# A two-layer graph network: host-laid edge lists and first weights, one load queue, the fallback branch at the end, products ahead of counts in the first row block

## The chip, the cores and the metric

The kernel runs on one core of a Trainium2 chip. The metric is the device time of one execution in microseconds; the median of three runs stands for the kernel. Profiles come from one further execution, whose own time is given beside its span.

## The reference

The inputs are 1250 nodes with 1024 features (x), 41250 edges (src, dst and one of two types; dst is sorted), and the weights. Two layers follow each other, each on h = relu(layernorm(x)) and each with a residual:

```python
h = max(layernorm(x), 0)
n = ln_weight * h * rsqrt(mean(h * h) + 1e-6)
y = n @ W_root + bias                          # 1024 x 286
for r in range(2):                             # two edge types
    w = (edge_type == r)
    y += segment_sum((n[src] @ W_rel[r]) * w, dst) / max(segment_sum(w, dst), 1)
x = x + h + elu(y) @ wo

h = max(layernorm(x), 0)
g = h @ W                                      # 1024 x 1024
e = exp(-leaky_relu((g @ a_l)[src] + (g @ a_r)[dst]))
x = x + elu(segment_sum(e * g[dst], src) / (segment_sum(e, src) + 1e-5))
```

## The kernel before

**Edges as counts.** Nothing is gathered. The edges, sorted by destination, are cut into NG = 110 chunks of J x 125 = 3 x 125 edges. Within a chunk the destinations span at most W = 16 nodes, so an edge is described by three numbers: the low seven bits of its source (`lows`), and a key that joins the source's tile of 128, the type, and the distance of its destination from the chunk's first one (`keys`). For each third of a chunk VectorE writes a one-hot matrix of the keys (`key`, line 505, 125 x 320); every second chunk it writes one of the low bits (`lo`, line 480). TensorE multiplies them (line 506) and so counts, in one PSUM bank for a chunk, the edges by source and by destination column. ScalarE copies the bank into the count matrix at a column that it loads from a table of first destinations (lines 511 to 513). An edge group that starts a new chunk at the previous chunk's last node is carried over by a small product (line 509) of one-hots `hot_ck` (line 487). Four PSUM banks serve the counts: three named `tp`, which the transposes share, and one of their own.

**Lists are prepared on the chip.** In `gnn_kernel` three loads of 110 rows x 375 entries come in on the queues of SP, ACT and POOL. VectorE finds each chunk's first and last destination, the step to the next chunk, and a number `odd` of chunks that break the assumption above; it forms keys, low bits and carries, and TensorE transposes them so that the edges of a chunk lie across partitions (lines 1204 to 1264). Then every engine loads `odd` into a register:

```python
n_odd = nc.values_load(info[0:1, NG:NG + 1], min_val=0, max_val=4 * NG + N)
with tc.If(n_odd == 0) as which:
    fast_arm(...)
with which.Else():
    general_arm(...)
```

The inputs here take the fast arm.

**Loads.** SP issues, after its list, x row block 0, then for each of 8 weight chunks the two relation matrices (one load) and the root matrix (another), with x row block 1 after chunk 3, then the other row blocks.

**Stage one of the fast arm.** The rows are cut into T = 10 blocks of 128. For a block t, `statistics` (line 528) and `norm` (line 541, ScalarE) form h, `turn` transposes eight tiles of it on TensorE (line 559), `scaled` copies them out of PSUM with the layer-norm weights (four on ScalarE, line 567, and four on VectorE, line 569), `square` (line 547) gives the second norm, `residual` adds h to x by a DMA of POOL. Sixteen products (line 648, 128 x 128 by 128 x 429, fp32, each two passes of the PE) take a block through two halves r of the three joined weight matrices, eight chunks k each. `first_part`, `second_part` and `third_part` bring the result of the block before to SBUF in three bf16 parts. The order on TensorE, VectorE and ScalarE is the program's own, since `manual_schedule` keeps them as written. Between two products `some(n)` advances the counts, so that all 330 key products are spread evenly over the 160 steps of the ten blocks:

```python
want = min(NG * J, ahead + -(-(NG * J - ahead) * (t * SK + i + 1) // (T * SK - 6)))
some(want - done)
```

Five of them (`ahead`) stand in front of the first product. In step i of block t stand also the preparation of blocks t + 1 and t + 2. The VectorE one-hots have five `key` buffers.

**Behind it** come the aggregation with the counts (line 719), the way back through wo (line 765), the second layer's product (lines 803 and 874), its edge weights (lines 947 and 950) and sums (lines 998 and 1011), and the output from line 969 on.

Of the kernel before, what the change touches and what calls it, by code (L numbers as in the profile page):

```python
# [30 lines left out]
J = 3  # L31
# [379 lines left out]
def fast_arm(tc, ctx, w_root, conv_bias, wo, w_gat, a_gat, out,  # L411
             ident, eps5, eps6, lnw, const, wt, wcat, bias, xs, cnt_raw,
             meta, keys, lows, hot_ck, ck, bases, iota_lo, iota_key, iota_ck):
# [56 lines left out]
    with ExitStack() as c1:  # L470
        hot = c1.enter_context(tc.tile_pool(name="hot", bufs=5))
        work = c1.enter_context(tc.tile_pool(name="work1", bufs=2))
# [17 lines left out]
        def chunks():  # L490

            for q in range(NG):
# [10 lines left out]
                for j in range(J):  # L503
                    key = hot.tile([PE_, 2 * T * W], BF16, name="key")
                    nc.vector.tensor_scalar(key, iota_key, keys[:, q, j:j + 1], None, op0=ALU.is_equal)  # L505
                    nc.tensor.matmul(acc[:, :2 * T * W], los[q // 2][:, :, (q % 2) * J + j], key, start=(j == 0),  # L506
                                     stop=(j == J - 1))
                    if q and j == 0:
                        nc.tensor.matmul(*carry, start=False, stop=False)
                    if j == J - 1:  # L510
                        b = nc.values_load(bases[0:1, q:q + 1], engines=[mybir.EngineType.Activation],
                                           min_val=0, max_val=N - 1)
                        nc.scalar.activation(cnt_w[:, :, bass.ds(b, W)], a3, AF.Copy)  # L513
                    yield
# [20 lines left out]
        def norm(t):  # L535
# [5 lines left out]
            nc.scalar.activation(h[:n], xs[t][:n], AF.Relu, bias=nmr[:n], scale=rstd[:n])  # L541
# [19 lines left out]
        def scaled(t, g):  # L561

            n, (hT, pts) = ROWS[t], hTs[t]
            for i in range(4):
                k = 4 * g + i
                if g == 0:
                    nc.scalar.activation(hT[:, k, :n], pts[g][:, i, :n], AF.Copy, scale=lnw[:, k:k + 1])
                else:
                    nc.vector.tensor_scalar(hT[:, k, :n], pts[g][:, i, :n], lnw[:, k:k + 1], None, op0=ALU.mult)
# [31 lines left out]

        for i in range(2):
            statistics(0, i)
        low_hots(0)
        carry_hots(0, 10)
        norm(0)
        some(4)
        for g in range(2):
            turn(0, g)
        scaled(0, 0)  # L610
        some(1)
        scaled(0, 1)
        done, ahead = 5, 5
        SK = 2 * KD
        for t in range(T):
            pys[t] = ps.tile([128, 2, 512], F32, name="mm")
            for i in range(SK):
                r, k = divmod(i, KD)
# [7 lines left out]
                if i == 6:  # L626
                    residual(t)
                if t == 0 and i in (1, 2):
                    statistics(1, i - 1)
                if t == 0 and i == 3:  # L630
                    norm(1)
                if t == 0 and i in (5, 7):
                    square(i // 6)
                if t + 2 < T:
                    if i in (6, 9):
                        statistics(t + 2, (i - 6) // 3)
                    elif i == 11:
                        norm(t + 2)
                    elif i == 13:
                        square(t + 2)  # L640
                if t + 1 < T:
                    if i in (8, 10):
                        turn(t + 1, i // 10)
                    elif i == 9:
                        scaled(t + 1, 0)
                    elif i == 12:
                        scaled(t + 1, 1)
                nc.tensor.matmul(pys[t][:ROWS[t], r, :F + HF], hTs[t][0][:, k, :ROWS[t]], wcat[k][:, r, :],  # L648
                                 start=(k == 0), stop=(k == KD - 1))
                want = min(NG * J, ahead + -(-(NG * J - ahead) * (t * SK + i + 1) // (T * SK - 6)))  # L650
# [459 lines left out]
def gnn_kernel(  # L1110
# [12 lines left out]
    a_gat: bass.AP,  # L1123
    out: bass.AP,
):
    nc = tc.nc
    D = x.shape[1]
    F = w_root.shape[1]
    HF = F // 2
    KD = D // 128  # L1130
    assert x.shape[0] == N and NG * GE == src.shape[0] and HF * 2 == F
# [4 lines left out]
    ident = const.tile([128, 128], F32, name="ident")  # L1136
    make_identity(nc, ident)
    ones = const.tile([128, 1], F32, name="ones")
    nc.vector.memset(ones, 1.0)
# [3 lines left out]
    nc.vector.memset(eps6, 1e-6)  # L1143
    lnw = const.tile([128, KD], F32, name="lnw")

    nc.scalar.activation(lnw[:, 0:1], eps5, AF.Sqrt)
    bias = const.tile([128, F], F32, name="bias")

    meta = const.tile([128, 2376], F32, name="meta")
    parts, at = [], 0  # L1150
    for size in (NG * J, NG * J // 2, NG * T, 3 * 128, T * W, T, NG, NG + 1):
# [5 lines left out]
    iota_lo = parts[3].bitcast(F16).rearrange("p (l j) -> p l j", j=2 * J)  # L1157
    iota_key, iota_ck, ck = parts[4].bitcast(F16), parts[5].bitcast(F16), parts[6]
    info = parts[7][0:1].bitcast(I32)

    xs = [big.tile([128, D], F32, name=f"x{t}", tag=f"x{t}") for t in range(T)]
    cnt_raw = big.tile([128, 2 * T * NPAD], F16, name="cnt")


    wt = [big.tile([128, D + 2], F32, name=f"w{k}") for k in range(KD)]
    wcat = [w[:, :3 * F].rearrange("p (r f) -> p r f", r=2) for w in wt]

    with ExitStack() as ec:
        ep = ec.enter_context(tc.tile_pool(name="ep", bufs=1))
        eps = ec.enter_context(tc.tile_pool(name="eps", bufs=2, space=PSUM))  # L1170
        eraw = ep.tile([NG, 3, GE], I32, name="eraw")
        for i, (a, eng) in enumerate(((dst, nc.sync), (src, nc.scalar), (etype, nc.gpsimd))):
            eng.dma_start(eraw[:, i, :], a.rearrange("(q e) -> q e", q=NG))
        lnw_row = ep.tile([KD, 128], F32, name="lnw_row")
        nc.scalar.dma_start(lnw_row, ln_w.rearrange("(k p) -> k p", p=128))
        nc.scalar.dma_start(bias, _bcast_rows(conv_bias, 128, F))

        def load_x(t):
            nc.sync.dma_start(xs[t][:ROWS[t]], x[t * 128:t * 128 + ROWS[t], :])

        load_x(0)
        for k in range(KD):
            ks = slice(k * 128, (k + 1) * 128)
            nc.sync.dma_start(wcat[k][:, :, :F], w_rel[:, ks, :].rearrange("r p f -> p r f"))
            nc.sync.dma_start(wcat[k][:, :, F:], w_root[ks, :].rearrange("p (r f) -> p r f", r=2))  # L1185
            if k == 3:
                load_x(1)
        for t in range(2, T):
            load_x(t)

        nc.gpsimd.iota(iota_lo, pattern=[[1, 128], [0, 2 * J]], base=0, channel_multiplier=0,
                       allow_small_or_imprecise_dtypes=True)
        nc.gpsimd.iota(iota_key, pattern=[[1, 2 * T * W]], base=0, channel_multiplier=0,
                       allow_small_or_imprecise_dtypes=True)
        nc.gpsimd.iota(iota_ck, pattern=[[1, 2 * T]], base=1, channel_multiplier=0,
                       allow_small_or_imprecise_dtypes=True)
        nc.gpsimd.memset(cnt_raw.rearrange("p (c n) -> p c n", n=NPAD)[:, :, N:], 0.0)


        end = ep.tile([NG, 1], F32, name="end")  # L1200
        nc.vector.tensor_scalar(end, ident[:NG, NG - 1:NG], N - 4096.0, 4096.0, op0=ALU.mult, op1=ALU.add)

        dstf = ep.tile([NG, GE], F32, name="dstf")
        nc.vector.tensor_copy(dstf, eraw[:, 0, :])
        first = ep.tile([NG, 1], F32, name="first")
        nc.vector.tensor_reduce(first, dstf, AX.X, ALU.min)
        below = ep.tile([NG, 1], F32, name="below")
        nc.vector.tensor_scalar_add(below, first, -4096.0)
        pn = eps.tile([128, 1], F32, name="pn", bufs=1)
        nc.tensor.matmul(pn[:NG], ident[:NG, 1:NG + 1], below, start=True, stop=True)  # L1210
        last = ep.tile([NG, 1], F32, name="last")
        nc.vector.tensor_reduce(last, dstf, AX.X, ALU.max)
        last2 = ep.tile([NG, 1], F32, name="last2")
        nc.vector.tensor_reduce(last2, dstf[:, :GE - PE_], AX.X, ALU.max)
        after = ep.tile([NG, 1], F32, name="after")
        nc.vector.tensor_tensor(after, pn[:NG], end, ALU.add)

        step = ep.tile([NG, 1], F32, name="step")
        nc.vector.tensor_tensor(step, after, first, ALU.subtract)
        odd = ep.tile([NG, 1], F32, name="odd")  # L1220
        nc.vector.tensor_scalar(odd, last, first, float(W), op0=ALU.subtract, op1=ALU.is_ge)
        nc.vector.scalar_tensor_tensor(odd, step, float(W), odd, op0=ALU.is_gt, op1=ALU.add)
        nc.vector.scalar_tensor_tensor(odd, last, after, odd, op0=ALU.is_gt, op1=ALU.add)
        nc.vector.scalar_tensor_tensor(odd, last2, after, odd, op0=ALU.is_ge, op1=ALU.add)
        pf = eps.tile([1, 128], F32, name="pf", bufs=1)
        nc.tensor.transpose(pf[:, :NG], first, ident[:NG, :NG])
        po = eps.tile([1, 1], F32, name="po", bufs=1)
        nc.tensor.matmul(po, odd, ones[:NG], start=True, stop=True)
# [73 lines left out]
```

## Time and profile before

| what | value |
|---|---|
| median of three runs | 631.08 us (630.55 to 632.11) |
| the profiled execution's time | 630.51 us |
| its span | 628.7 us |
| TensorE busy | 607.1 us, 97% |
| VectorE busy | 390.8 us, 62% |
| ScalarE busy | 182.9 us, 29% |
| loads and stores | 30.18 MB, mean 48 GB/s |

A busy share is the share of the span in which the engine had an instruction running. Matmuls are pipelined, so their busy times overlap, and the distance between starts tells more. A row of the timeline gives start, length, engine, line, operation, the tile written and the tiles read; in square brackets stand the idle time before it and what ended that. In a row of waits stand total, times and longest, in microseconds.

### The profile page before, as it was taken

The numbers are of one execution on the slowest core, as the hardware profiler recorded it, in microseconds if no ns is written. First come the engines' busy times: TensorE is split into PE (matmuls) and PEld (weight loads), VectorE is DVE, ScalarE is ACT, GpSimd is POOL, SyncE is SP. The second block draws the span as 40 slices with busy tenths as digits, with TensorE's granted clock in tenths as the row PEclk, the third lists the DMA queues.
The fourth block names the chain that finished last, engine by engine and source line by source line (L and its number), as shares of the span: only waits on it lengthen the run. The fifth ranks groups of instructions, "written<-read, shape, count | busy, mean of one in ns | idle before, by whom it ended". The sixth has DMA issues, their size and how long they took to land.

```text
span 628.7 us, 7874 instructions
## 1 busy us (share of the span) xinstructions
PE 607.1 (97%) x2816; PEld 415.1 (66%) x2816; DVE 390.8 (62%) x945; ACT 182.9 (29%) x348; POOL 43.0 (7%) x53
## 2 busy tenths in 40 slices
PE   2999999999999999999999999999999999999995
PEld 1566666666666767667667888888766666666653
DVE  6788888889772766569876231215445556666532
ACT  2555555555533000014312132222122112222211
POOL 3100000000000000000000000010010011111110
PEclk9999999999999999999999999999999999999999
DMA  7961111011106600000090000000000000000001
GB/s 229 266 198 35 33 35 30 6 34 34 27 1 223 211 1 1 0 1 2 4 200 7 2 2 0 1 0 1 1 0 33 34 33 34 33 34 34 33 35 31
DMA packets 26633, 30.18 MB, mean 48 GB/s; under 512 B 14405, under 2 KB 19068, under 8 KB 26584
## 3 DMA queue, kind: packets, MB, share of 16 engines
q1 hardware_dynamic: 24815, 23.98, 12.7%
q0 software_dynamic: 1488, 5.29, 4.4%
q8 instruction: 24, 0.39, 0.3%
q10 hardware_dynamic: 281, 0.32, 0.2%
q14 instruction: 25, 0.20, 0.1%
HBM read 16.06 MB, written 5.12 MB: 34 GB/s over the span
## 4 chain that ended last, share of the span: by engine, by line
PE 94%; DMA 3%; SPq 1%; DVE 1%; ACT 0%; issue 0%
PE mm L648 18%; PE mm L998 16%; PE mm L874 11%; PE mm L719 11%; PE p L998 8%; PE acc L506 7%; PE mm L765 5%; PE z L874 4%; PE mm L803 3%; PE p L1011 3%; DMA w<-in_L_gnn_W_rel_dram 2%; PE p L803 1%; PE tp L559 1%; DMA x<-in_x_dram 1%; PE mm L766 1%; SPq L1185 1%
## 5 line engine op out<-in xcount | busy, mean ns | idle before, releaser
L648 PE MATMUL mm<-w,hT 128*128 128x429 f32 (+1 forms) x320 | 144.5, 535 | 0.0
L998 PE MATMUL mm<-h,z 128*128 128x342 f32 (+1 forms) x360 | 118.5, 450 | 0.0
L505 DVE TENSOR_SCALAR key<-meta 125x320 bf16<-125x320 f16 x330 | 85.3, 299 | 21.0 <-PE acc L506 10.5
L998 PEld LDWEIGHTS mm<-h,z 128*128 128x128 f32 (+1 forms) x360 | 68.4, 190 | 34.9
L506 PEld LDWEIGHTS <-lo 125*128 125x128 bf16 x330 | 40.8, 126 | 58.1 <-issue 38.1
L506 PE MATMUL acc<-key,lo 125*128 125x320 bf16 x330 | 74.2, 305 | 4.9 <-DVE key L505 4.9
L719 PE MATMUL mm<-y,cnt 128*128 128x286 bf16 (+3 forms) x600 | 74.9, 284 | 0.2 <-DVE y L600 0.2
L513 ACT ACTIVATE cnt<-acc 128x320 f32 x110 | 49.9, 453 | 80.1 <-PE acc L506 71.2
L719 PEld LDWEIGHTS <-cnt 128*128 128x128 f16 (+1 forms) x600 | 59.3, 99 | 14.4 <-issue 0.8
L998 PE MATMUL p<-h,z 128*128 128x341 f32 (+1 forms) x180 | 66.1, 449 | 0.0
L648 PEld LDWEIGHTS mm<-w,hT 128*128 128x128 f32 (+1 forms) x320 | 51.1, 190 | 3.3 <-issue 2.1
L998 PEld LDWEIGHTS p<-h,z 128*128 128x128 f32 (+1 forms) x180 | 33.7, 188 | 17.7
L874 PE MATMUL mm<-w,a 128*128 128x257 f32 (+3 forms) x192 | 44.8, 380 | 0.0
L874 PEld LDWEIGHTS mm<-w,a 128*128 128x128 f32 (+1 forms) x192 | 35.6, 187 | 6.0 <-ACT h L900 0.4
L765 PE MATMUL mm<-wo,meta 128*128 128x512 f32 (+1 forms) x80 | 37.6, 592 | 0.0
L967 POOL TENSOR_TENSOR w<-w,x 128x1024 f32<-128x1024 f32 x9 | 23.4, 2599 | 135.3 <-ACT w L963 120.7
L947 DVE SCALAR_TENSOR_TENSOR z<-z 128x1280 f32<-128x1280 f32 (+2 forms) x11 | 31.2, 2843 | 0.3
L988 DVE TENSOR_SCALAR inv<-mm 128x1 f32<-128x1 f32 x9 | 1.4, 159 | 47.7 <-PE mm L998 47.7
L480 DVE TENSOR_TENSOR lo<-meta 125x768 bf16<-125x768 f16 x55 | 30.2, 548 | 0.0
L950 ACT ACTIVATE z<-z 128x1280 f32<-128x1280 f32 (+2 forms) x11 | 12.9, 1173 | 58.7 <-DVE z L949 58.7
L963 ACT ACTIVATE w<-mm,inv 128x684 f32<-128x684 f32 x9 | 7.5, 832 | 74.3 <-DVE w L962 74.3
L730 ACT ACTIVATE bias<-bias 128x286 f32<-128x286 f32 (+1 forms) x10 | 4.4, 443 | 79.9 <-DVE bias L729 79.9
(181 smaller groups left out, 726.3 us busy)
## 6 DMA issues: line engine op xcount, KB each, us to landing
x<-in_x_dram SPq DMA_DIRECT2D x9, 512.0 KB, 4.9
x<-h POOLq DMA_DIRECT2D x9, 512.0 KB, 4.6
out_dram<-w SPq DMA_DIRECT2D x9, 512.0 KB, 3.0
w<-in_L_gnn_W_dram SPq DMA_DIRECT2D x8, 512.0 KB, 5.0
w<-in_L_gnn_W_rel_dram SPq DMA_DIRECT2D x8, 286.0 KB, 6.7
w<-in_L_gnn_W_root_dram SPq DMA_DIRECT2D x8, 143.0 KB, 4.9
a<-in_L_gnn_a_dram SPq DMA_DIRECT2D x2, 512.0 KB, 5.5
wo<-in_L_gnn_wo_weight_dram SPq DMA_DIRECT2D x2, 512.0 KB, 9.7
```

The lines of the kernel that those rows point to most:

```text
L480: nc.vector.tensor_tensor(los[q // 2], iota_lo, lows[:, q:q + 2, :].rearrange("p q j -> p (q j)")[:, None, :].to_broadcast([PE_, 128, 2 * J]),
L505: nc.vector.tensor_scalar(key, iota_key, keys[:, q, j:j + 1], None, op0=ALU.is_equal)
L506: nc.tensor.matmul(acc[:, :2 * T * W], los[q // 2][:, :, (q % 2) * J + j], key, start=(j == 0), stop=(j == J - 1))
L513: nc.scalar.activation(cnt_w[:, :, bass.ds(b, W)], a3, AF.Copy)
L648: nc.tensor.matmul(pys[t][:ROWS[t], r, :F + HF], hTs[t][0][:, k, :ROWS[t]], wcat[k][:, r, :], start=(k == 0), stop=(k == KD - 1))
L719: nc.tensor.matmul(pm[:n, r, :f], cnt[:k, h, r, t * 128:t * 128 + n], ybs[h][:k, s, r, :f], start=(h == 0 and s == 0), stop=(h == T - 1 an ...
L765: nc.tensor.matmul(po[:n, c, :], oT[:, i, :n], wo_of[i][:, cs], start=(i == 0), stop=False)
L803: nc.tensor.matmul(o, hT[:, k, :n], wg[k][:, c0:c1], start=(k == 0), stop=(k == KD - 1))
L874: nc.tensor.matmul(o[:a.shape[2], :c1 - c0], a[:, k, :], b[k][:, c0:c1], start=(start and k == 0), stop=(k == KH - 1), skip_group_check=no ...
L947: nc.vector.scalar_tensor_tensor(z, z, 0.1, z, op0=ALU.mult, op1=ALU.min)
L967: nc.gpsimd.tensor_add(high, high, xs[s][:n].rearrange("p (h c) -> p h c", h=2))
L998: nc.tensor.matmul(o, z[:ROWS[t], t, :n], hs[t][:ROWS[t], c0:c1], start=(t == 0), stop=(t == T - 1))
```

## The change

On the host (`_laid_out`), the three lists are stacked and laid out by chunk position: 128 (125 used) x 3 x 110 x 3. Each chunk's first destination is taken as a list of 110, the relation and root matrices are joined by columns into one 1024 x 858 array, and the layer-norm weights are laid out as 128 x 8.

In the kernel, all large loads go through SP: x block 0 in two halves, weight chunk 0, the lists, the first destinations (to all partitions), chunks 1 to 3, x block 1, chunks 4 to 7, the bias, the other x blocks. The identity is made after one iota, and twelve products of the identity with itself are issued first on TensorE, into the count bank. x block 0 is normalized first; the key decode follows on VectorE with edges already across partitions. Block 0's products run chunk by chunk (both halves r in turn) and the counts start with the sixth product. All eight scalings of a block are on ScalarE. The number of odd chunks is formed in block 2; if it is above 0, ScalarE clears the counts there, and after the fast arm the general arm is run over the result.

```diff
 def fast_arm(...)
+        room = [yh.tile([128, F + 3 * (F + 2)], F32, name=f"room{t}", tag=f"yh{t}") for t in (9, 8, 7)]
+        rows = room[0][:, :3 * NG * J].bitcast(I32).rearrange("p (i q j) -> p i q j", i=3, j=J)
+        idle = own_bank("idle")
+        for _ in range(12):
+            nc.tensor.matmul(idle[:, 0, :], ident, ident, start=True, stop=True)
+        loads(0)
+        nc.sync.dma_start(rows, edges)
+        nc.sync.dma_start(firsts_at, _bcast_rows(firsts, 128, NG))
+        loads(1)
...
-                if g == 0:
-                    nc.scalar.activation(hT[:, k, :n], pts[g][:, i, :n], AF.Copy, scale=lnw[:, k:k + 1])
-                else:
-                    nc.vector.tensor_scalar(hT[:, k, :n], pts[g][:, i, :n], lnw[:, k:k + 1], None, op0=ALU.mult)
+                nc.scalar.activation(hT[:, k, :n], pts[g][:, i, :n], AF.Copy, scale=lnw[:, k:k + 1])
...
         for i in range(2):
             statistics(0, i)
-        low_hots(0)
-        carry_hots(0, 10)
         norm(0)
-        some(4)
+        nc.vector.tensor_scalar(tile_of, raw[:, 0], 7, None, op0=ALU.logical_shift_right)
+        nc.vector.scalar_tensor_tensor(block, tile_of, 2.0, raw[:, 1], op0=ALU.mult, op1=ALU.add)
+        nc.vector.tensor_tensor(d, raw[:, 2], first[:, :, None].to_broadcast([PE_, NG, J]), ALU.subtract)
+        nc.vector.scalar_tensor_tensor(keys, block, float(W), d, op0=ALU.mult, op1=ALU.add)
         for g in range(2):
             turn(0, g)
-        scaled(0, 0)
-        some(1)
-        scaled(0, 1)
-        done, ahead = 5, 5
+        for g in range(2):
+            scaled(0, g)
+        nc.vector.scalar_tensor_tensor(lows, tile_of, -128.0, raw[:, 0], op0=ALU.mult, op1=ALU.add)
+        low_hots(0)
+        def count_over():
+            nc.vector.tensor_tensor(over, d, limit, ALU.subtract)
+            nc.vector.scalar_tensor_tensor(over, d, -1.0, over, op0=ALU.mult, op1=ALU.max)
...
+            nc.vector.tensor_reduce(worst[:PE_], over, AX.XY, ALU.max)
+        def clear_if_odd():
+            odd = nc.values_load(n_odd, engines=[mybir.EngineType.Activation], min_val=0, max_val=8192)
+            with tc.If(odd > 0):
+                nc.scalar.activation(cnt_raw, eps6.to_broadcast([128, 2 * T * NPAD]), AF.Copy, scale=0.0)
+        first_plan = {
+            6: lambda t: carried(),
+            8: lambda t: statistics(1, 0),
+            9: lambda t: statistics(1, 1),
+            10: lambda t: norm(1),
+            11: lambda t: square(0),
+            12: lambda t: (residual(0), turn(1, 0)),
+            13: lambda t: (scaled(1, 0), turn(1, 1)),
+            14: lambda t: statistics(2, 0),
+            15: lambda t: (statistics(2, 1), scaled(1, 1)),
+        }
+        late_plan = {(1, 1): lambda: square(1), (1, 2): lambda: norm(2), (1, 12): lambda: square(2),
+                     (2, 1): lambda: count_over(), (2, 4): lambda: turn_worst(), (2, 6): lambda: worst_over(),
+                     (2, 12): lambda: clear_if_odd()}
+        done, late = 0, 5
...
-                r, k = divmod(i, KD)
+                r, k = divmod(i, KD) if t else (i % 2, i // 2)
...
-                want = min(NG * J, ahead + -(-(NG * J - ahead) * (t * SK + i + 1) // (T * SK - 6)))
+                want = min(NG * J, -(-NG * J * max(t * SK + i + 1 - late, 0) // (T * SK - 6 - late)))
 def gnn_kernel(...)
+    def loads(part):
+        if part == 0:
+            for c in (slice(0, 512), slice(512, D)):
+                nc.sync.dma_start(xs[0][:, c], x[:128, c])
+        for k in range(1) if part == 0 else range(1, KD):
+            nc.sync.dma_start(wt[k][:, :3 * F], w_cat[k * 128:(k + 1) * 128, :])
+            if k == 3:
+                load_x(1)
...
-    n_odd = nc.values_load(info[0:1, NG:NG + 1], min_val=0, max_val=4 * NG + N)
-    with tc.If(n_odd == 0) as which:
...
+    odd = nc.values_load(n_odd, min_val=0, max_val=8192)
+    with tc.If(odd > 0):
```

`carried` holds the step between chunks, the limits (three operations on POOL) and the carry one-hots; the plan of blocks 1 to 9 is that of before.

## The prediction

> **What bounds the kernel now.** I read the page's busy shares and slices first, then the PE's waits, the timeline of the opening, the chain that ended last, and windows over stages.
>
> ```profile
> PE 607.1 (97%) x2816; PEld 415.1 (66%) x2816; DVE 390.8 (62%) x945; ACT 182.9 (29%) x348; POOL 43.0 (7%) x53
> PE   2999999999999999999999999999999999999995
> PEclk9999999999999999999999999999999999999999
> ```
>
> TensorE is at nine tenths or more in every slice but the first (15.7 us a slice) and the last. A change to the opening can be paid at most what the first slice and the holes just behind it lose. The PE's waits name that loss:
>
> ```profile
> PE pn L1210 <- DVE below L1208: 7.5, 1, 7.5
> PE acc L506 <- DVE key L505: 4.9, 4, 3.5
> ```
>
> They cover the list decode on VectorE and the first one-hot keys. The timeline shows what is serial there:
>
> ```profile
> 4.68 0.93 DVE L1204 CAST dstf<-eraw 110x375 f32<-110x375 int32 x1 [3.76 <-DMA eraw<-in_dst_dram]
> ...
> 12.14 0.15 DVE L1232 TENSOR_TENSOR meta<-po,info_f 1x1 int32<-1x1 f32 x1 [0.69 <-PE po L1228]
> ...
> 13.04 1.29 DVE L528 BATCH_NORM_STATS2 st<-x 128x6 f32<-128x512 f32 x2 [0.75 <-DMA w<-in_L_gnn_W_root_dram]
> ...
> 15.58 1.24 ACT L541 ACTIVATE h<-x,nmr,rstd 128x1024 f32<-128x1024 f32 x1 [0.68 <-DVE nmr L539]
> ...
> 16.95 1.93 PE L559 MATMUL tp<-ident,h 128*128 128x128 f32 x8
> ...
> 18.86 0.88 PE L648 MATMUL mm<-w,hT 128*128 128x429 f32 x2
> ```
>
> The lists are decoded until 12.3 us, then the branch is decided on their verdict, and only then do the statistics of x0 start, though x0 has long been there (below). The first useful product with weights is at 18.86 us. The chain gives the end of the first row block (16 products, each two rows of the trace) and of the stage:
>
> ```profile
> 38.18 0.81 PE mm L648 x2
> ```
>
> ```profile
> 192.79 4.34 PE mm L648 x12
> ```
>
> So block 0 ends at 39.0 us and the stage at 197.1: nine blocks in 158.1 us, 17.6 each. In that stretch the other engines have room (window 39.1 to 197.1, groups by line):
>
> ```profile
> 39.10:197.10 158.00, 158.00 (x744) 96.79 (x743) 130.24 (x441) 81.07 (x184) 6.62 (x8) 1.00 0.17 35
> ```
>
> ```profile
> L505 DVE TENSOR_SCALAR key<-meta 125x320 bf16<-125x320 f16 x288 | 75.1, 300 | 20.4 <-PE acc L506 9.9 <-PE acc L509 7.9
> L513 ACT ACTIVATE cnt<-acc 128x320 f32 x99 | 44.9, 453 | 73.5 <-PE acc L506 67.1 <-PE acc L509 3.0 <-PE mm L648 1.6
> ```
>
> The columns after the length are PE, PEld, DVE, ACT, POOL: VectorE 82%, ScalarE 51%, both waiting for the PE and not the PE for them. The last product ends near 621.5 us; the 7 us behind it (last evictions, output, end) are touched only by the branch.
>
> **The change part by part.** The sum is made by one question: when is row block 0 done, and how much of the later work has been done by then?
>
> *Loads.* Before, three list loads on three queues precede x0. Now SP issues x0 in two halves, weight chunk 0, lists, first destinations, chunks 1 to 3, x1, chunks 4 to 7, bias, x2 and on. Bytes: x0 0.52 MB, a chunk 0.44, lists 0.51, firsts 0.06. The windows of one microsecond show 20, 196 and 348 GB/s up to 4 us and 348, 332, 339, 204, 344 from 3 to 8 us, mean 313. So 0.56 MB are moved by 4.0 us. From last byte to landing I take 1.3 us: the first relation weights of before had 1.46 MB up to and with them (lists, x0, bias, themselves), a sum that the windows reach near 7.1 us, and landed at 8.34. Hence x0 lands at 5.2 us (first half 4.4), chunk 0 at 6.5, lists at 8.1, firsts at 8.3, chunk 7 (5.1 MB in all) at 19.8, x2 at 22. SP issues one load in 0.4 to 0.6 us and holds eight in flight; a load waits for the one eight before it, and by these landings the ring never runs empty. The small lnw load stays on ACT's queue and is needed only at 8.2 us; the bias, moved behind chunk 7, lands near 20 us and is needed at about 28.
>
> *h first.* After the second half: statistics 0.68, then as in the trace from the end of the statistics (14.33) to nmr without the two VectorE instructions that stood between, 1.0 us: h's first half starts at 6.9. A half costs 0.65 (1.24 for the whole): 7.55 and 8.2. Transposes of 4 start at 7.6.
>
> *Twelve identity products*, 24 passes on the PE, from about 1.9 us (the identity follows one 0.43 us iota on POOL). Row: the first eight transposes took 1.93 us, and their weight loads 1.61, which is 0.20 each; a later four took 0.44 from start to next work, 0.11 each, although the granted clock reads 1.00 throughout. [...]
>
> *Products first.* ScalarE, after h, scales eight tiles of 0.285 us from 8.25 on; the first product goes at 8.55, and two products on each chunk (now in turn, chunk by chunk) cost 2 x 0.72. Six products take 8.55 to 12.9; chunks 1 and 2 land at 9.7 and 11.1, in time. Then ten products (7.4), 25 key products and their carries (0.145 each, 3.6), eight transposes (0.9), small gaps 0.3: the PE would end block 0 at 25.1.
>
> *Decode on VectorE* from 8.15, now laid by chunk so that no transposes are needed: shift 0.75 (0.84 for 375 columns, now 330), four more of about 0.48, low hots 0.5: keys from 11.2, three by 12.0. Carry work 1.1 us. From 13.1 to key 25: 22 keys x 0.235, 4 low hots x 0.5, 4 statistics x 0.65, and 1.2 of small ones, 11 us: 24.1. PE and VectorE are nearly level, so neither hides the other fully; I put the end of block 0 at 25.5 (24.5 to 28).
>
> *Sum of the opening.* Before, at 39.0, 5 + 34 = 39 key products were done; now 25. The 14 missing cost 14 x 0.145 = 2.0 later. Gain 39.0 - 2.0 - 25.5 = 11.5 us. In steady blocks 35.4 in place of 33.8 keys a block add VectorE 0.6, but VectorE gives up four scalings (1.1) to ScalarE; the two end at 80% and about 59%. Cover is ample: zero.
>
> *Verdict on the lists.* Moved from before everything to block 2: on VectorE two 330-wide operations, a reduction (the 375-wide one took 0.52) and small ones, 1.9 us; then a PE transpose (0.11) and two small ones. Behind them on VectorE are keys; five buffers hold 5/35 of a block, 2.5 us, so it costs between 0 and 2; I take 0.4, since the buffers are not always full. SP's read of the verdict stands ahead of the attention weight loads, which waited 161.7 us for the PE anyway: free. POOL's three limit operations and a copy lie beside the first residual add, on an engine 7% busy: free.
>
> *Branches.* In block 2 every engine passes a jump, ScalarE a register load and a compare. Row: VectorE's load, compare and next start took from 12.29 to 13.04, 0.75. On ScalarE this is hidden (49% idle; its evictions have four banks). On the PE only the jump counts. [...] At the end a compare replaces a jump; VectorE's 0.75 there lies beside the last output's landing: 0 (ends -0.5 and 1).
>
> Total: 11.5 - 0.4 - 0.3 - 0.3 (ScalarE's later eviction, below) = 10.5. The profiled run took 630.5 (span 628.7), so 620.0 by it; the median of the runs, 631.1, stands 0.6 higher, so 620.5.
>
> **Rivals.**
> *The loads pace block 0.* If the ring moves 200 to 230 GB/s (before's first ten microseconds had 206), chunk 7 lands at 25 to 28, and with the last two steps of 1.1 each block 0 ends at 27.3 to 30.2: 622 to 625.5. For: before stalled on SP and loads until 26.9 in the chain. Against: rows are now 3.4 and 4 KB, where before had 0.6 and 1.1 KB, and 10 us of x loads moved 309 GB/s.
> *VectorE late in block 0 and 2.* Lists 2 us late, and the verdict's full 2: about 624. This is also the way in which the change doesn't do what it says: products first, then waiting for keys.
> *Slower: ScalarE keeps PSUM banks.* Steps 11 to 13 of each block now queue h (1.24), four scalings (1.13) and the square (1.3); evictions between them wait, and with them the bank of the second transposes. From 1.3 us of PE stall in each of nine blocks it eats the gain; at 1.7 the time is 635. For: a clump of 3.7 us in 3.3 us of steps. Against: in a steady block h ended at 106.1 and the next eviction came at 106.55, the one after at 107.79; scaling to 107.2 delays one by 0.7 us, and three shared banks and one own turn over every 1.4 us. Hence 0.3 in the sum.
>
> **How the numbers follow.** Likeliest case 0.72 (617.5 to 622.5); loads 0.10; VectorE 0.10; slower 0.06; a balance of mishaps that leaves no change 0.02. What can be told from no change is 0.3%, 1.9 us. Best end: block 0 at 24.5 with nothing lost behind, 12.5 us, and x0 landing 1 us sooner: 617.0. Upper end, taking in the two middle cases: 625.5. Faster 0.92, same 0.02, slower 0.06.
>
> **What would show it.** First weight product at 8 to 10 us; transposes before it at 0.11 each (identities right) or 0.2 (wrong); first keys at 11 to 12.5; block 0 done near 25.5 and the stage at about 186; last product near 611. A PE wait on weight loads in the first 25 us is the first rival; on keys beyond 1 us the second; on ScalarE's evictions from block 1 on the third. A hole of over 1 us in the PE at the jump in block 2 would make the branch term wrong. An end of block 0 past 30 us, or a stage longer than 162 us behind it, would make the prediction wrong.

## The result and the profile after

| | median | lowest to highest | runs |
|---|---|---|---|
| before | 630.82 us | 630.15 to 632.11 | 4 |
| after | 620.35 us | 620.33 to 620.36 | 4 |

The ratio is 0.983 (0.9815 to 0.985): 10.5 us less. The profiled execution took 620.34 us with a span of 618.4. The page's busy rows and TensorE's slices, kernel after:

```profile
PE 607.4 (98%) x2828; PEld 416.7 (67%) x2828; DVE 379.6 (61%) x899; ACT 191.0 (31%) x385; POOL 45.1 (7%) x56
PE   8999999999999999999999999999999999999995
```

TensorE's first slice went from 2 tenths to 8. Not all of that is useful work: the twelve identity products (line 481) fill 5.2 us of it. The timeline of the opening, kernel after:

```profile
1.67 5.18 PE L481 MATMUL idle<-ident 128*128 128x128 f32 x24 [1.67 <-POOL ident masks.py:199]
3.74 1.35 DVE L542 BATCH_NORM_STATS2 st<-x 128x6 f32<-128x512 f32 x2 [0.97 <-DMA x<-in_x_dram]
6.10 1.52 ACT L557 ACTIVATE h<-x,nmr,rstd 128x512 f32<-128x512 f32 x2 [0.42 <-DVE nmr L553]
6.96 1.36 PE L575 MATMUL tp<-ident,h 128*128 128x128 f32 x8
8.16 1.63 PE L720 MATMUL mm<-w,hT 128*128 128x429 f32 x4
9.72 0.50 DVE L626 TENSOR_TENSOR room<-room,meta 125x330 f32<-125x330 int32 x1 [0.81 <-DMA meta<-in_firsts_dram]
10.90 3.12 PE L720 MATMUL mm<-w,hT 128*128 128x429 f32 x8 [1.11 <-DMA w<-in_w_cat_dram]
11.76 0.72 DVE L519 TENSOR_SCALAR key<-meta 125x320 bf16<-125x320 f16 x3
13.86 0.57 PE L520 MATMUL acc<-key,lo 125*128 125x320 bf16 x3
```

Statistics start at 3.74 instead of 13.04 us, the first product with weights at 8.16 instead of 18.86, and the first key product now stands behind six weight products. What is new is in the brackets: VectorE waits 0.81 us for the first destinations, and the PE 1.11 us for weight chunk 1. The PE's waits on weights, in total, times and longest, kernel after:

```profile
PE mm L720 <- DMA w<-in_w_cat_dram: 1.4, 2, 1.1
```

The decode's 7.5 us and the keys' 4.9 are gone. The chain shows block 0's last product, and in another stretch the end of the stage, kernel after:

```profile
25.53 0.72 PE mm L720 x2
...
182.27 4.34 PE mm L720 x12
```

Block 0 ends at 26.3 us (39.0 before) and the stage at 186.6 (197.1 before), 10.5 us sooner. From there to the last product both kernels take the same: 621.5 - 197.1 = 424.4 before, 611.0 - 186.6 = 424.4 after. The tail behind the last product went from 7.2 to 7.4 us. So the whole difference is made in block 0, and 2.2 us of it are given back in the nine blocks behind it (160.3 us in place of 158.1). Which part of the early start is owed to the host's lists and which to normalizing first was not separated: no run takes out one of the two alone, so the timeline's starts are what shows them.

### The profile page after: what moved, and what is told of

Same layout as the page of the kernel before. It is cut to its first block, busy times and chain, and to the rows that moved or that the text cites. A ratio compares the mean times of both kernels' runs of the same rounds, so it can differ in the third digit from the quotient of the medians.

```text
span 618.4 us, 7877 instructions
## 1 busy us (share of the span) xinstructions
PE 607.4 (98%) x2828; PEld 416.7 (67%) x2828; DVE 379.6 (61%) x899; ACT 191.0 (31%) x385; POOL 45.1 (7%) x56
## 3 DMA queue, kind: packets, MB, share of 16 engines
q1 hardware_dynamic: 22070, 24.53, 12.7%
## 4 chain that ended last, share of the span: by engine, by line
PE 95%; DMA 2%; SPq 1%; DVE 0%; ACT 0%; issue 0%
PE mm L720 18%; PE mm L1070 17%; PE mm L946 11%; PE mm L791 11%; PE p L1070 8%; PE acc L520 7%; PE mm L837 6%; PE z L946 4%; PE mm L875 3%; PE p L1083 3%; DMA w<-in_w_cat_dram 2%; PE p L875 1%; PE tp L575 1%; PE mm L838 1%; PE tp L910 1%; PE tp L926 1%
## 5 line engine op out<-in xcount | busy, mean ns | idle before, releaser
L520 PE MATMUL acc<-key,lo 125*128 125x320 bf16 x330 | 72.2, 303 | 0.0
L1022 ACT ACTIVATE z<-z 128x1280 f32<-128x1280 f32 (+2 forms) x11 | 12.9, 1173 | 58.8 <-DVE z L1021 58.8
```

## The experiments

The times in this section are medians of four to twelve runs. The kernel before, which ran beside them, had 630.4 to 630.7 us.

**What each part of the opening is worth.**

`r_outer`: block 0's products again go through half 0 of all chunks, then half 1.

```diff
-                r, k = divmod(i, KD) if t else (i % 2, i // 2)
+                r, k = divmod(i, KD)
```

> The changed kernel with block 0's products in the old order (all eight chunks for the first half, then for the second). If the arrival of the chunks paces block 0, product 7 must wait for chunk 7, near 21.3 us, and eight more steps of 1.1 us and the transposes follow: block 0 ends near 31.3 us, 625.3 us (624 to 626.5). If the PE or VectorE paced it, below 621 us.

Measured 629.04 us, ratio 0.997 (0.996 to 0.999): nearly all of the gain is gone, 8.7 us lost where 5 were expected, and above the expected range. Waits and timeline of this kernel:

```profile
PE mm L720 <- DMA w<-in_w_cat_dram: 6.0, 3, 2.5
```

```profile
19.24 1.77 PE L720 MATMUL mm<-w,hT 128*128 128x429 f32 x2 [2.53 <-DMA w<-in_w_cat_dram]
21.61 1.64 PE L720 MATMUL mm<-w,hT 128*128 128x429 f32 x2
...
34.03 0.89 PE L720 MATMUL mm<-w,hT 128*128 128x429 f32 x2
```

One product on each chunk as it comes is 0.72 us of work for a load of some 1.1 us (0.44 MB at the 418 GB/s of after from 19 to 20 us), so the PE waits 4.6 us longer than after. That much was expected. More stands in the second column: behind three waits of 1.95, 1.48 and 2.53 us two products take 1.77 and 1.64 us instead of 0.9, and the third 1.26. The array is at half rate, and here the granted clock says so, at 0.50; it is the third figure from the end of a window, of this kernel:

```profile
19.00:24.00 5.00, 4.76 (x11) 2.50 (x12) 2.24 (x7) 0.44 (x1) 0.00 (x0) 0.50 1.04 419
24.00:25.00 1.00, 1.00 (x5) 0.40 (x4) 0.83 (x3) 0.00 (x0) 0.00 (x0) 0.82 1.00 410
```

In windows of 0.2 us the clock falls near 17.5 us, 0.8 us into the third wait, and returns near 24.4. In the first transposes of before the weight loads had taken 0.20 us as well, but with a granted clock of 1.00. The 5.1 us from 19.24 on at half rate cost about 2.5 us (an estimate), so 7.1 of the 8.7 us are accounted for and 1.6 are not. Product 16 starts at 34.03 instead of 25.37 us, 8.7 later, and the median is 8.7 higher. The order by chunks is thus the part on which the others rest: an early start is worth something only where each byte that lands brings enough work.

`no_idle`: the kernel after without the identity products.

```diff
-        idle = own_bank("idle")
-        for _ in range(12):
-            nc.tensor.matmul(idle[:, 0, :], ident, ident, start=True, stop=True)
```

> The changed kernel without the twelve identity products. [...]

Measured 621.09 us, ratio 0.985 (0.983 to 0.987). Timeline of this kernel:

```profile
6.95 1.94 PE L572 MATMUL tp<-ident,h 128*128 128x128 f32 x8 [6.95 <-ACT h L554]
8.68 2.11 PE L717 MATMUL mm<-w,hT 128*128 128x429 f32 x4
11.21 3.12 PE L717 MATMUL mm<-w,hT 128*128 128x429 f32 x8 [0.42 <-DMA w<-in_w_cat_dram]
```

The eight transposes start at the same time and take 1.94 us instead of 1.36, and the first four passes 2.11 instead of 1.63. So with the identities ahead of them they are faster. But the wait for chunk 1 shrinks from 1.11 to 0.42 us: a PE that came sooner would only have waited longer. Of about 1.0 us that this costs, 0.3 reach the end of block 0 (product 16 starts at 25.66 instead of 25.37) and of the stage (186.9 instead of 186.6). The median is 0.7 higher; the rest of it is not in this trace's opening. Its tail is 7.7 us instead of 7.4, at work that the edit doesn't touch.

`half_dve`: half of the scalings go back to VectorE in every block.

```diff
-                nc.scalar.activation(hT[:, k, :n], pts[g][:, i, :n], AF.Copy, scale=lnw[:, k:k + 1])
+                if g == 0:
+                    nc.scalar.activation(hT[:, k, :n], pts[g][:, i, :n], AF.Copy, scale=lnw[:, k:k + 1])
+                else:
+                    nc.vector.tensor_scalar(hT[:, k, :n], pts[g][:, i, :n], lnw[:, k:k + 1], None, op0=ALU.mult)
```

> The changed kernel with four of a block's eight scalings back on VectorE. If the PE alone bounds the blocks after the first, the two engines' room decides nothing: 620.3 us (620.0 to 620.7). If relief of VectorE carries part of the gain (1.1 us a block), 621.5 us or more; if ScalarE's clump costs PSUM banks, below 620.0.

Measured 621.39 us, ratio 0.985 (0.984 to 0.987): 1.0 more than after. VectorE in the opening of this kernel:

```profile
11.06 1.12 DVE L585 TENSOR_SCALAR hT<-tp,lnw 128x128 f32<-128x128 f32 x4
...
13.17 0.72 DVE L519 TENSOR_SCALAR key<-meta 125x320 bf16<-125x320 f16 x3
```

Four scalings of 1.12 us in all stand ahead of the first keys, which come at 13.17 instead of 11.76. Product 16 starts at 26.27 (25.37 after) and the stage ends at 187.6 (186.6 after): the loss is there at the end of block 0, and nine steady blocks add 0.1. Not all of the 0.9 us need be the scalings: in this execution the first destinations also landed 0.4 later (VectorE goes on at 10.10 instead of 9.72), which the edit doesn't touch. Which of the two engines scales matters only in the one block where VectorE has the decode before it.

`counts_from_3rd`: the counts begin with the third product, and the carries' preparation moves with them.

```diff
-        done, late = 0, 5
+        done, late = 0, 2
...
-            6: lambda t: carried(),
+            3: lambda t: carried(),
```

> The changed kernel with counts from the third product on (and the carry work at step 3). If VectorE's first keys (11.8 us, and the carry one-hots near 13.5) are later than the third product (11.6 us), the PE waits 0.5 to 1.5 us for them in block 0: 621.0 us (620.6 to 621.8). If keys are in time, the spread is the same work in another order: 620.3 us.

Measured 622.5 us, ratio 0.9875 (0.986 to 0.989), 2.1 more than after and above the expected range. Its PE waits on keys:

```profile
PE acc L520 <- DVE key L519: 0.8, 2, 0.6
```

The keys aren't there yet and the PE stands before them; the stage ends at 188.0, 1.4 later than after. That is more than the wait. The first product also starts 0.4 later in this execution (8.58 instead of 8.16), ahead of anything that the edit touches, and the rest isn't explained.

**Loads.**

`before_wcat`: the kernel before, with the two loads of a chunk joined into one of the host-laid array, and nothing else.

```diff
-            nc.sync.dma_start(wcat[k][:, :, :F], w_rel[:, ks, :].rearrange("r p f -> p r f"))
-            nc.sync.dma_start(wcat[k][:, :, F:], w_root[ks, :].rearrange("p (r f) -> p r f", r=2))
+            nc.sync.dma_start(wt[k][:, :3 * F], w_cat[k * 128:(k + 1) * 128, :])
```

> The kernel before with the joined weights alone: one load of 3.4 KB rows for each chunk in place of two with 1.1 and 0.6 KB rows, and eight issues fewer on SP. If the list decode on VectorE holds the opening, little moves, only the hole behind x2's landing at 26.9 us closes: 630.0 us (629.4 to 630.5). If the loads held it as much, 628 us or less.

Measured 630.39 us, ratio 0.9995 (0.9986 to 1.0004): nothing. Its PE still has the wait of before on the first keys:

```profile
PE acc L506 <- DVE key L505: 3.5, 1, 3.5
```

`packed`: in the kernel after, the first destinations are 110 more columns of the edge list, laid by the host for each partition, so that one load brings both.

```diff
-        nc.sync.dma_start(rows, edges)
-        nc.sync.dma_start(firsts_at, _bcast_rows(firsts, 128, NG))
+        nc.sync.dma_start(lists, edges)      # 128 x (3 * NG * J + NG)
```

> The changed kernel with the first destinations as 110 more columns of the list array, in one load of 4400-byte rows; same bytes. If the separate load of 128 rows of 440 bytes stalls the ring (123 and 187 GB/s at 7 to 9 us) and so holds the decode by 0.8 us and weight chunk 1 by 1.1 us, block 0 ends near 25.4 us and the time is 619.5 us (619.0 to 619.9). If only bytes count, chunk 1 lands as before: 620.2 us.

Measured 619.59 us, ratio 0.9825 (0.981 to 0.984), 0.8 less than after, though the same bytes are moved. Windows of one microsecond, the last column GB/s and the one before it the share of the DMA engines; first the kernel after, then `packed`:

```profile
7.00:8.00 1.00, 0.95 (x7) 0.71 (x8) 0.00 (x0) 0.96 (x3) 0.00 (x0) 1.00 0.52 123
8.00:9.00 1.00, 1.00 (x6) 0.66 (x5) 0.84 (x2) 1.00 (x6) 0.00 (x0) 1.00 0.56 187
```

```profile
5.00:6.00 1.00, 1.00 (x7) 1.00 (x6) 0.57 (x4) 0.29 (x1) 0.00 (x0) 1.00 0.57 100
...
7.00:8.00 1.00, 1.00 (x7) 1.00 (x7) 0.00 (x0) 0.58 (x1) 0.00 (x0) 1.00 1.03 412
8.00:9.00 1.00, 0.98 (x7) 0.57 (x5) 0.48 (x2) 0.95 (x4) 0.43 (x1) 1.00 1.00 405
```

In the kernel after, the load of the first destinations, 128 rows of 440 B out of one row of 440 B in memory, stands in the same queue ahead of chunks 1 to 3, and around it the DMA engines are busy for only 0.52 and 0.56 of two microseconds. `packed` has one such microsecond too, at 5 us (0.57); by 9 us it has moved 2.18 MB and after 1.80. Without the small load the products of block 0 begin later and never stop, and the last one starts at 24.59 instead of 25.37 (timeline of `packed`):

```profile
8.47 4.59 PE L720 MATMUL mm<-w,hT 128*128 128x429 f32 x12
...
24.59 0.89 PE L720 MATMUL mm<-w,hT 128*128 128x429 f32 x2
```

What in that load is slow (the small rows, the one source row, or a pause of the queue around it) these runs don't separate.

`list_act`: the same two list loads of the kernel after, issued from ScalarE's queue.

```diff
-        nc.sync.dma_start(rows, edges)
-        nc.sync.dma_start(firsts_at, _bcast_rows(firsts, 128, NG))
+        nc.scalar.dma_start(rows, edges)
+        nc.scalar.dma_start(firsts_at, _bcast_rows(firsts, 128, NG))
```

> The changed kernel with the lists and first destinations issued by ScalarE's queue instead of SP's, fourth and fifth. If the order of bytes in one queue matters, lists and x0 share the engines from the start: x0's landing moves 1 us back (statistics from about 4.7 us instead of 3.7), the decode starts up to 2 us sooner but cannot use it behind the statistics: 620.9 us (620.3 to 621.8). If only SP's issue time matters, the chunks come about 0.9 us sooner: 619.7 us.

Measured 621.11 us (620.05 to 622.04), ratio 0.985 (0.983 to 0.987), which cannot be told from after. Its timeline:

```profile
5.62 0.69 DVE L542 BATCH_NORM_STATS2 st<-x 128x6 f32<-128x512 f32 x1 [1.23 <-DMA x<-in_x_dram]
...
9.38 3.07 PE L720 MATMUL mm<-w,hT 128*128 128x429 f32 x8
```

With the lists in a queue of their own the first destinations are there by 7.45 us (9.72 after), x block 0's second half comes 1.2 us late (the wait of 1.23), and the first product starts at 9.38 instead of 8.16. That the two queues share the engines is the author's reading of this. From there on the PE doesn't wait for weights. What is won behind is lost in front; by this run the one queue is worth having for its order.

**Verdict and branches.**

`before_no_branch`: the kernel before, without its branch; the general arm is left out.

```diff
-    n_odd = nc.values_load(info[0:1, NG:NG + 1], min_val=0, max_val=4 * NG + N)
-    with tc.If(n_odd == 0) as which:
-        fast_arm(...)
-    with which.Else():
-        general_arm(...)
+    fast_arm(...)
```

> The kernel before without its branch: the general arm is left out, the verdict is still formed. If the gain is the whole serial opening (lists decoded on VectorE ahead of x0), the branch alone gives back the 0.75 us between verdict and first statistics and little more, since VectorE still has the same list: 629.5 us (629.0 to 630.5). If waiting for the verdict on every engine was the main cost, at least half of the 10.5 us goes: 626 us or less.

Measured 627.10 us, ratio 0.994 (0.992 to 0.996), between the two expectations, and for neither's reason. In the opening the first product comes 1.4 us sooner (17.44 instead of 18.86), but at the end of the stage only 0.3 are left. Two waits in its block 0, one on a root load and one on the low one-hots, take most of it back:

```profile
27.62 0.96 PE L648 MATMUL mm<-w,hT 128*128 128x429 f32 x2 [0.32 <-DMA w<-in_L_gnn_W_root_dram]
...
33.14 0.30 PE L506 MATMUL acc<-key,lo 125*128 125x320 bf16 x1 [0.45 <-DVE lo L480]
```

The tail gives another 2.5 us: from the last product (614.71 + 6.49 = 621.2) to the end of the span (625.9) it has 4.7 us, where before has 7.2. The queues in the last stretch of the span (packets, MB, share of the DMA engines), first of before, then of `before_no_branch`:

```profile
q14 instruction: 6, 0.05, 1.9%
q8 instruction: 2, 0.03, 1.5%
```

```profile
q1 hardware_dynamic: 322, 0.23, 8.9%
```

With the branch, eight packets of instructions (0.08 MB) are fetched while the kernel ends; without it, none. The profiled execution was the slowest of the four (627.66), so this accounts for 2.8 us and not for the whole 3.4 of the medians.

`no_verdict`: the kernel after without verdict, without the branch in block 2 and without the one at the end; the general arm is left out.

```diff
-                     (2, 1): lambda: count_over(), (2, 4): lambda: turn_worst(), (2, 6): lambda: worst_over(),
-                     (2, 12): lambda: clear_if_odd()}
...
-    odd = nc.values_load(n_odd, min_val=0, max_val=8192)
-    with tc.If(odd > 0):
-        general_arm(...)
```

> The changed kernel with the verdict on the lists, the branch in block 2 and the branch at the end left out (so is the general arm). If the far jump at the end is what made the kernel before 3.4 us faster without its branch (its tail behind the last product fell from 7.2 to 4.7 us, and the instruction packets of the tail disappeared), the tail here falls from 7.4 to about 4.7 us and block 2 gives at most 0.2 more: 617.7 us (617.4 to 618.0). If the forecast's terms hold instead (0.4 for the verdict, 0.3 for the jump in block 2, nothing at the end): 619.6 us.

Measured 617.01 us, ratio 0.978 (0.9765 to 0.980), 3.3 less than after. Its last product ends at 605.80 + 4.61 = 610.4 us and the span at 615.0, a tail of 4.6 instead of 7.4:

```profile
605.80 4.61 PE L1082 MATMUL p<-h,z 128*98 128x448 f32 x26
```

So 2.8 of the 3.3 us are in the tail. Of the other 0.5, some 0.4 are there before block 0 ends (chunk 1 is waited for 0.8 us instead of 1.1), ahead of anything that was taken out: a difference between two executions. Little over 0.1 is left for the verdict and the jump in block 2.

The rows of the final branch in the kernel after (shortest, median and longest in ns, first and last start) say where the tail's time goes:

```profile
L1277 SPq COMPARE_BRANCH  x1: 53/53/53, 613.2 to 613.2; - x1
L1277 SPq EVENT_SEMAPHORE  x9: 17/17/17, 616.1 to 616.7; - x9
```

SP's branch takes 0.05 us, and its next instruction comes 2.9 us after the branch began. VectorE has the same gap at its own time (branch at 612.5, next at 615.4), and has it in before too (622.5, 625.4), where no register is loaded ahead of that jump. So the load isn't the price. That the gap is the fetch of instructions is argued from the packets.

`early_jump`: the whole computation, on `packed`. The three output stores of the last row block move into an Else branch, so that SP comes to its jump while the PE is still at work.

```diff
-        nc.sync.dma_start(out[...], lo)
+        finals.append((out[...], lo))
...
-    with tc.If(odd > 0):
+    with tc.If(odd > 0) as which:
         general_arm(...)
+    with which.Else():
+        for o, lo in finals:
+            nc.sync.dma_start(o, lo)
```

> The version with packed first destinations (619.6 us), with the last row block's three output stores moved into an else branch of the final test: SP compares and jumps while the PE still works on the last row block, and runs off the end of the program behind its last store. If the far jump's instruction fetch is the cost of the tail: 617.2 us (616.9 to 617.7). If the tail is paid for another reason (closing the program, the stores' landing): 619.5 us.

Measured 618.27 us, ratio 0.980 (0.978 to 0.981): 1.3 less than `packed`, 2.1 less than after and 12 less than before, the best of the kernels that keep the whole computation. The last product ends at 605.76 + 4.61 = 610.4 us and the span at 617.0: the tail is 6.6 us in the profiled execution, the slowest of the four (618.93), so not all of the 2.8 came back. SP now takes its jump at 599.6 us. VectorE still comes to its own behind its last work, and SP waits 1.5 us for it:

```profile
L1278 DVEq COMPARE_BRANCH  x1: 76/76/76, 611.9 to 611.9; - x1
L1278 DVEq EVENT_SEMAPHORE  x2: 21/21/21, 614.7 to 614.8; - x2
```

What an earlier jump of VectorE would bring was not tried.

## Why the prediction was right, point by point

It gave 620.5 us (617.0 to 625.5); 620.35 were measured. The mechanism is the one it named, and none of the rivals came about. Several terms of the sum were off, and that they cancel to 0.15 us is luck: block 0 ended 0.8 later, the nine blocks lost 2.2 instead of 3.0, the tail and the time outside the span added 0.3, and the 0.5 put on for a median above the profiled execution didn't come (620.35 and 620.34).

- **Loads, "the ring never runs empty": wrong.** The step that failed is the landing of the firsts, put at 8.3. The lists came at 8.0, as predicted (8.1); the firsts landed near 9.7, chunk 1 at 10.9 instead of 9.7, because the ring moved only 123 and 187 GB/s around the small load. `packed` puts the price at 0.8 us. From 9 to 14 us the ring is better than predicted (383 to 421 GB/s instead of 313), and the later chunks cost one wait of 0.3 us. This was the first rival's mechanism in a small measure (1.4 us of waits in all) and not at its price.
- **x0 and h first:** statistics began at 3.74 instead of 4.4 us and h at 6.1 instead of 6.9, since x0 landed sooner than the lag of 1.3 us allowed.
- **Identities, transposes at 0.11 us each (0.2 if they fail):** right, 0.105 each (four weight loads in 0.42 us). That they leave no loss at all, as the sum has it, rested on no trace and is shown by no run; what the runs show is 1.36 us for the eight transposes with the identities (after) and 1.94 without (`no_idle`). The granted clock reads 1.00 over the slow transposes of before and over the fast ones of after, so it doesn't tell. Without them 0.3 us are lost at the end of block 0 and 0.7 in the median, because the wait for chunk 1 covers part. `r_outer` shows half rate with a granted clock of 0.50: its longest wait was 2.53 us, and the clock fell 0.8 us into it.
- **Products first, six from 8.55 to 12.9:** they began at 8.16, 0.4 sooner, and ended at 13.86, 1.0 late; in between lies the wait of 1.1 for chunk 1.
- **Keys from 11.2:** they came at 11.76, after the 0.8 us wait for the firsts, and in time: no PE wait on keys is among the waits of after. The second rival (VectorE late) didn't come about.
- **End of block 0, put at 25.5:** 26.3, the mis-sized term, and the excess lies ahead of the counts: from the end of the sixth product on, the prediction's own working gives 25.1 - 12.9 = 12.2 us and the trace 26.3 - 13.9 = 12.4.
- **Counts left for later, 2.0 us:** the nine blocks took 160.3 us instead of 158.1, so 2.2.
- **Verdict 0.4, jump in block 2 0.3, ScalarE's evictions 0.3, 1.0 in all:** too dear. What the nine blocks lost beyond the counts is 0.2. The 0.3 for the jump was the author's estimate, and no run shows it. Not every engine passes a jump in block 2, as was thought: in the trace ScalarE alone has the branch, it takes 0.05 us, and around it the chain on the PE goes on without a hole:

```profile
L674 ACTq COMPARE_BRANCH  x1: 50/50/50, 59.4 to 59.4; - x1
```

```profile
58.62 0.72 PE mm L720 x2
59.34 0.14 PE acc L520
59.48 0.02 PE acc L523
```

- **ScalarE and VectorE have room:** in the stretch from block 1 to the stage's end VectorE is busy 129.4 of 160.2 us (81%) and ScalarE 95.1 (59%), the predicted shares. The columns after the length are again PE, PEld, DVE, ACT, POOL; kernel after:

```profile
26.30:186.50 160.20, 160.20 (x763) 98.79 (x762) 129.35 (x438) 95.09 (x230) 7.65 (x11) 1.00 0.21 48
```

- **Branch at the end, 0:** right as a difference (tail +0.2 us), but not as it was thought. The branch at the end costs 2.5 us of tail in before and 2.8 in after; the change swaps one for the other. The prediction saw only VectorE's register load there; the trace of after shows 2.9 us from SP's branch to SP's next instruction.

The sum against the profile: 12.7 us sooner at the end of block 0 (39.0 - 26.3), 2.2 given back, 0.2 in the tail and 0.1 outside the span: 10.2, as between 630.5 and 620.3.

## What to carry to other kernels

When a kernel waits in its opening, starting sooner is half of the change: the work must be ordered so that each load that lands brings at least its own time in products (here two products a chunk instead of one decided 8.7 of 10.5 us). Look at the tail with the same care, at the instruction fetches in the list of queues and at the rows of the branch itself: a branch behind the last work cost 2.5 and 2.8 us here, which the waits of TensorE, VectorE and ScalarE don't show. And compare single executions with care: the same opening loads landed up to 0.4 us apart in kernels whose edits don't touch them. When terms are summed, split the opening by what lands when, since one small load in the same queue can set the pace (0.8 us here, by `packed`).

## What the runs showed of the hardware

- A branch that skips a large arm at the end of the program went with 2.5 us more of tail (before against `before_no_branch`) and 2.8 us (after against `no_verdict`), and with eight packets of instructions, 0.08 MB, in the tail. The branch itself took 0.05 us on SP (after, at 613.2); the next instruction came 2.9 us after its start. ScalarE's branch in block 2, which skips one instruction, took 0.05 us and left no hole in TensorE's work.
- Around one load of 56 KB, 128 rows out of one row in memory, the queue moved 123 and 187 GB/s for two microseconds, where 412 and 405 were moved in the same two without it; by 9 us the difference was 0.38 MB.
- After waits of 1.95, 1.48 and 2.53 us within ten microseconds TensorE's granted clock read 0.50 from about 17.5 to 24.4 us, and the products behind the last wait took 1.77, 1.64 and 1.26 us instead of 0.9. A single wait of 1.1 us in the kernel after left it at 1.00.
- In these openings the granted clock was no sign of the rate: it read 1.00 where eight transposes took 1.93 us (before, from 16.95 us) and where they took 1.36 (after, from 6.96 us).
